# A decoder layer on one core: a third pair of feed-forward blocks by two levels of Strassen products, and down's weight sums made by accumulating loads

## The chip, the cores and the metric

The kernel runs on one core of a Trainium2 chip. The metric is the device time of one execution in microseconds (us). The kernel before has a median of 2212.78 us over three runs (2210.60 to 2213.64). The profile is of one execution that took 2210.64 us; its span, from the first to the last profiled instruction, is 2208.9 us.

The engines are TensorE (PE; its weight loads are listed as PEld), VectorE (DVE), ScalarE (ACT), GpSimd (POOL) and SyncE (SP). DMAs are issued by SP, POOL and ACT, each from a queue of its own that is served in order.

## The reference

Input x is 16 batches of 128 tokens by 1024 channels in float32. Three residual steps follow each other, each on a layer norm of x:

```python
x = x + _L0_attn_ref(_layernorm(x), Wqkv, bqkv, Wo, bo)             # self attention, width 256
x = x + _L0_xattn_ref(_layernorm(x), ctx, ctx, Wq, Wk, Wv, Wo, ...) # 8 heads of 64
x = x + _L0_ffn_ref(_layernorm(x), gate, up, down ...)              # 1024 -> 2752 -> 1024
# the last one:
Wg, Wu, Wd = dequantize(gate...), dequantize(up...), dequantize(down...)
h = silu(x @ Wg.T) * (x @ Wu.T)
return h @ Wd.T
```

The three weights of the last step are packed as two 4-bit numbers per byte, with a scale and a zero for each group of 64, and are taken out as `(w - zero) * scale`. This step is most of the work.

## The kernel before, in words

**Stages.** Self attention runs to about 249 us of the span, cross attention to about 750 with a tail of small pieces up to about 802 that lies among the products of the first feed-forward block. Then comes gate and up for the second half of the batches ("pass 0", to 1266), gate and up for the first half ("pass 1", to 1728.5), and the down stage for all tokens (to 2200.7).

**Blocks.** The 2752 inner columns are ten full blocks of 256 (0 to 9) and a last one, RB = 10, of 192. A pass has 1024 tokens.

**One level.** `one_block` (L1205, with `products`, L1167) multiplies a block by a Strassen-Winograd scheme: halves of the block's columns, of the 1024 channels and of the tokens, so 7 products for gate and 7 for up in place of 8 each. A product is four matmuls of 128x128 by 512 columns. The seven sums of weights are made beforehand (`prepare`) and stored in device memory; the seven sums of tokens (`T`) lie in SBUF.

**Two levels.** `two_levels` (L1414) takes two neighbouring blocks, a pair, and applies the scheme once more inside each of the seven outer products: 49 multiplies for a pair, gate and up together, each four matmuls of 128x128 by 256 columns. The inner sums of weights (`li`) are made by GpSimd (`inner_left`, L1392), the inner sums of tokens (`ti`) by VectorE (`inner_right`, L1362), and results are combined by VectorE from PSUM (`got`). In pass 0, `PAIRS = [3, 4]` (L1095): blocks 0 to 5 go by one level, then pairs 3 and 4 (blocks 6 to 9) by two. In pass 1 all five pairs go by two levels. RB goes by one level in both passes.

**Preparation.** `prepare` (L215 to L296) is a generator that unpacks weights: it loads raw bytes, splits the nibbles, subtracts the zero, multiplies by the scale (tile `pa`, 128x1024, two buffers), makes four combinations with VectorE (`comb`, tile `pc`) and stores seven 256 KB tiles per block and matrix. For down, the matrix "d" of a block, it makes four combinations too (L275 to L284) and stores all seven sums, in the order DOWN, which is also the order of the outer products of the down stage: 1, 2, 6, 5, 3, 7, 4. Steps of the generator are taken by hand: function `beside` (L1631 to L1664) is called at each of a one-level block's fourteen products, and `between` at each outer product of a pair. Raw loads and stores go by a `Route` (L55), whose engine is changed by hand: GpSimd's queue from the start of the feed-forward, SP's from the start of the last one-level block before the pairs.

**Order.** The order of work on an engine is that of the code, except that helpers of class `InOrder` (L65) pin their own instructions among each other and a scheduler places the others around them by priority. The trace gives all instructions of such a helper one line, L73, so tiles are told by name.

**Cross attention's moves.** Query tiles are turned by VectorE (`kt`), written by SP to device memory (`kd`, L856) and read back in another layout by SP (`qs`, L861); normalised rows are written to `xt` (`turn_rows`, L589). `project_out` multiplies by `qs`, takes squares (`sq`) on ScalarE, adds them up on TensorE (`mm<-sq,ones`), and VectorE makes the norm (`y<-sq,y`) and adds it to X. VectorE's chain is in order, so `h<-p,k` of block 0 stands behind it.

**The down stage.** For each of seven outer products `oq`, `operands` (L1026) loads by SP the sums of h (`lq`) and, by `load_right` (L1037), the sums of down's weights: for kc = 0 the five even blocks (pool wq0, 5 buffers), for kc = 1 the odd ones (pool wq1, 10 buffers). `remainder` (L1746) loads RB's (`wr`). They are prefetched while the outer product before is multiplied. `combine` (L1756) makes inner sums on VectorE (`lc`, `wc`): sums of number 5 need the even tiles alone, at inner product 7 of the outer product before; number 6 the odd ones too, at inner product 3; number 7 both. The inner order is 1, 5, 6, 7, 3, 4, 2, and VectorE's results `iu` and `iv` free the PSUM banks of 6 and 5. `got` (L1788) adds up.

Of the kernel before, what the change touches and what calls it, by code (L numbers as in the profile page):

```python
# [18 lines left out]
P = 128  # L19
# [19 lines left out]

GATE = (1, 7, 6, 2, 5, 4, 3)  # L40
DOWN = (1, 2, 6, 5, 3, 7, 4)
BLOCKS = [(b * 2 * P, min(P, (INTER - b * 2 * P) // 2)) for b in range(-(-INTER // (2 * P)))]


# [32 lines left out]
def decoder_layer(  # L77
# [137 lines left out]
    def prepare(jobs, ahead, queue, vector=nc.vector, sync=nc.sync, loads_first=False):  # L215


        units = [(blk, mat, s) for blk, mat in jobs for s in range(1 if mat == "r" else 2)]
        loads = deque(load_raw(*u, sync) for u in units[:ahead])
        stores = deque()  # L220
        if loads_first:
            yield

        def put():
            while stores:
                queue.dma_start(*stores.popleft())

        for k, (blk, mat, s) in enumerate(units):
            size = [BLOCKS[blk][1] if mat == "d" else P, 512]

            if s == 0:
                A = {}
            put()
            raw, scale, zero = loads.popleft()
            if k + ahead < len(units):
                loads.append(load_raw(*units[k + ahead], sync))

            pair = pools["a"].tile([P, 2, 512], F32, name="pa")[: size[0]]
            for n, ops in enumerate(
                (  # L240
                    (4, 15, ALU.logical_shift_right, ALU.bitwise_and),
                    (15, None, ALU.bitwise_and),
                )
            ):
                A[(n, s) if mat == "d" else (s, n)] = pair[:, n]
                nib = pair[:, n].bitcast(I32)
                vector.tensor_scalar(
                    nib if mat == "d" else nib.rearrange("p (j f) -> p j f", j=JC), raw, *ops
                )
            if mat != "d":  # L250
                pair = pair.rearrange("p n (j f) -> p (n j) f", f=P)
            vector.tensor_tensor(pair, pair.bitcast(I32), zero, ALU.subtract)
            vector.tensor_tensor(pair, pair, scale, ALU.mult)
            yield
            if mat == "r":
                out = wprep[blk, mat] = dram.tile([2, *size], F32, name="wr0", tag="wr0")
                for n in range(2):
                    stores.append((out[n], A[0, n]))
            if s == 0:
                continue  # L260
            put()
            out = wprep[blk, mat] = dram.tile(
                [7, *size], F32, name=f"w{mat}{blk}", tag=f"w{mat}{blk}"
            )

            def store(q, t):
                stores.append((out[(DOWN if mat == "d" else GATE).index(q)], t))

            def comb(a, b, op):
                t = pools["c"].tile([P, 512], F32, name="pc")[: size[0]]  # L270
                vector.tensor_tensor(t, a, b, op)
                return t

            store(1, A[0, 0])
            if mat == "d":  # L275
                store(3, A[1, 1])
                store(2, A[1, 0])
                put()
                t1 = comb(A[0, 1], A[0, 0], ALU.subtract)
                store(5, t1)  # L280
                t2 = comb(A[1, 1], t1, ALU.subtract)
                store(6, t2)
                store(7, comb(A[1, 1], A[0, 1], ALU.subtract))
                store(4, comb(A[1, 0], t2, ALU.subtract))  # L284
            else:
                store(4, A[1, 1])
                store(2, A[0, 1])
                put()
                s1 = comb(A[1, 0], A[1, 1], ALU.add)
                store(5, s1)  # L290
                s2 = comb(s1, A[0, 0], ALU.subtract)
                store(6, s2)
                store(7, comb(A[0, 0], A[1, 0], ALU.subtract))
                store(3, comb(A[0, 1], s2, ALU.subtract))
            yield
        put()  # L296

# [252 lines left out]

    tensor, vector = InOrder(tc, nc.tensor), InOrder(tc, nc.vector)
    sync = InOrder(tc, nc.sync)

# [35 lines left out]
    def turn_rows(b, xn, pool):  # L589

        kt = pool.tile([P, 4, 2 * JC, Q], F32, name="kt")
        vector.transpose(
            kt.rearrange("p c m t -> p m c t"), xn.rearrange("p m (c i) -> p m c i", c=4)
        )
        xt = xt_all[PASSES.index(b - b % HB)][b % HB]
        for a in range(4):
            sync.dma_start(
                xt[a].rearrange("c i n j t -> i c (n j t)"),
                kt[ts(a, Q)].rearrange("i c m t -> i c (m t)"),
            )  # L600
# [53 lines left out]
    if True:  # L654
# [163 lines left out]
        def query_unit(b, pair, qs, wait):  # L818
# [26 lines left out]
            def turn():  # L845
                kt = bkt.tile([P, 4, NB, Q], F32, name="kt")
                vector.transpose(
                    kt.rearrange("p c n j -> p n c j"),
                    qe.rearrange("p h d -> p (h d)").rearrange("p (n c j) -> p n c j", c=4, j=Q),
                )  # L850
                kd = dram.tile([4, Q, 4, NB, Q], F32, name="kd", tag="kd", bufs=3)
                sync.dma_start(kd.rearrange("a i c n j -> (a i) c n j"), kt)

                def load():
                    qt = qs[pair] = bqs.tile([P, 4, NB, Q], F32, name="qs", tag="qs")
                    for c in range(4):  # L856
                        sync.dma_start(
                            qt[ts(c, Q)], kd[:, :, c].rearrange("a i n j -> i a n j")
                        )

                later(1, load)  # L861
# [174 lines left out]

    def load_right(oq, kc, wb):  # L1037
        for i in range(NI):
            t = wb[kc, i] = pools[f"wq{kc}"].tile([P, 512], F32, name="wq")
            nc.sync.dma_start(t, wprep[2 * i + kc, "d"][DOWN.index(oq)])  # L1040

    def direct(lb, wb, L, W):

# [12 lines left out]
    with ExitStack() as gs:  # L1056
# [18 lines left out]
            banks.append(pool("c_u", 4, space=PSUM, side="right"))  # L1075

        cxb = rest = None
        route.engine = nc.gpsimd
        flagged = []


# [10 lines left out]
            return [[(2 * i + f, mat, q) for mat in "gu"] for q in DOWN for f in range(2)]  # L1092


        PAIRS = [3, 4]  # L1095
        order = [blk for blk in range(RB) if blk // 2 not in PAIRS]
        order.insert(2 * PAIRS[0], None)
        to_load = deque([t for blk in order[: 2 * PAIRS[0]] for t in tiles_of(blk)])
# [315 lines left out]
        def two_levels(ps, pairs, operands, between=lambda i, q: None):  # L1414
# [13 lines left out]
            def do_extra(n, more=0):  # L1428
                for todo, k in ((right, n), (extra, more)):
                    for _ in range(min(k, len(todo))):  # L1430
                        todo.popleft()()

            state = {}
            hs = {}
            sums = {}
# [98 lines left out]
            for n, (i, q) in enumerate(OUTERS):  # L1534
# [22 lines left out]
                if ps == 0 and q == 3:  # L1557
                    extra.extend(operands.inner_right(OUTERS[n + 2][1]))
                if ps == 1 and n == 0:
                    extra.append(lambda: outer_operand(operands.T, 4))  # L1560
                elif ps == 1 and n == 4:
                    extra.extend(operands.inner_right(4))
                multiply(n, 2)
                got(n, (0, 0), 2, 1)
                multiply(n, 5)
# [65 lines left out]
        def beside(n, mat, q):  # L1631
# [35 lines left out]
        for blk in order:  # L1667
            if blk is None:
# [11 lines left out]
                T1.update({1: pass1[0, 0], 2: pass1[1, 0], 3: pass1[1, 1]})  # L1680
                continue
            if blk == 2 * PAIRS[0] - 1:
                route.engine = nc.sync
# [31 lines left out]
    with ExitStack() as dst:  # L1715
# [30 lines left out]
        def remainder(oq):  # L1746
# [41 lines left out]
        def got(oq, ib, src, add=None, extra=None):  # L1788
# [11 lines left out]
            if oq == 4 and add is None:  # L1800

                for i in range(BPT):
                    v(m[:, i], src[:, i], u[:, i], ALU.add)
                    bs, cols = place(oq, ib)
                    outs.append((out[bs.start + i, :, cols], m[:, i]))
                    put_outs(nc.scalar if i % 2 == 0 else nc.sync)
# [10 lines left out]
            else:  # L1817
                if oq == 7:
                    v(u, src, u, ALU.add)
                v(m, src, w if oq in (3, 7) else u, ALU.add)  # L1820
            if add is not None:
                if oq == 5:
                    p(w, w, u, ALU.add)
                elif oq in (6, 7):
                    p(u, u, m, ALU.add)
                if oq in (3, 7):
                    p(m, m, w, ALU.add)
                elif oq == 2:
                    p(m, m, u, ALU.add)
                elif oq == 4:  # L1830
                    v(m, m, u, ALU.add)
            if xt is not None:
                p(m, m, xt, ALU.add)
            if oq in (2, 3, 7, 4):
# [142 lines left out]
```

## Time and profile before

| what | us |
|---|---|
| median of three runs | 2212.78 |
| the profiled execution | 2210.64 |
| its span | 2208.9 |
| TensorE busy | 2186.6 (99%), granted clock 0.999 |
| VectorE busy | 1499.2 (68%) |
| GpSimd busy | 667.4 (30%), 0.00 in the down stage |
| ScalarE busy | 510.4 (23%) |
| pass 0, one-level blocks 1 to 5 | 240.33 |
| pass 0, two pairs | 171.4 |
| pass 1, five pairs | 424.7 |
| down stage, seven outer products | 472 |
| DMA, mean share of 16 engines, 800 to 1000 / down stage | 0.94 / 0.52 |

The stages' times are differences of starts in the chain of waits, which follows the end of the program back through what released each piece of work; it runs along TensorE nearly all the time (94%). "Landing" is the time from the issue of a DMA to its completion. Busy engines are given over the whole span; what an engine costs is only to be seen in what TensorE waits for.

### The profile page before, as it was taken

The numbers are of one execution on the slowest core, as the hardware profiler recorded it, in microseconds if no ns is written. First come the engines' busy times: TensorE is split into PE (matmuls) and PEld (weight loads), VectorE is DVE, ScalarE is ACT, GpSimd is POOL, SyncE is SP. The second block draws the span as 40 slices with busy tenths as digits, with TensorE's granted clock in tenths as the row PEclk, the third lists the DMA queues.
The fourth block names the chain that finished last, engine by engine and source line by source line (L and its number), as shares of the span: only waits on it lengthen the run. The fifth ranks groups of instructions, "written<-read, shape, count | busy, mean of one in ns | idle before, by whom it ended". The sixth has DMA issues, their size and how long they took to land.

```text
span 2208.9 us, 24417 instructions
## 1 busy us (share of the span) xinstructions
PE 2186.6 (99%) x8500; PEld 1546.9 (70%) x8500; DVE 1499.2 (68%) x2055; ACT 510.4 (23%) x688; POOL 667.4 (30%) x646
## 2 busy tenths in 40 slices
PE   8999999999999999999999999999999999999998
PEld 7556555555555544444888588888887788888887
DVE  6897578888887767764578668667676645554462
ACT  2111235665566441111121112122211000000000
POOL 5453134333333335551344234444442000000000
PEclk9999999999999999999999999999999999999999
DMA  6435447777896788996566736566575966334631
GB/s 255 160 130 188 138 143 244 221 234 232 238 296 198 222 268 273 321 316 213 189 250 231 218 131 209 174 212 206 176 229 191 330 197 197 100 118 140 213 119 40
DMA packets 257716, 450.43 MB, mean 204 GB/s; under 512 B 27632, under 2 KB 122352, under 8 KB 254384
## 3 DMA queue, kind: packets, MB, share of 16 engines
q1 hardware_dynamic: 214944, 351.23, 49.8%
q0 software_dynamic: 24336, 78.40, 10.6%
q10 hardware_dynamic: 18304, 19.14, 2.8%
q8 instruction: 70, 1.15, 0.2%
q14 instruction: 62, 0.51, 0.1%
HBM read 281.35 MB, written 166.79 MB: 203 GB/s over the span
## 4 chain that ended last, share of the span: by engine, by line
PE 94%; DVE 3%; issue 1%; ACT 0%; POOL 0%; DMA 0%; DVEq 0%; POOLq 0%
PE q L73 26%; PE po L1856 21%; PE p L73 14%; PE kq L73 10%; PE mm L73 8%; PE kx L73 5%; PE mm L412 4%; PE mm L427 2%; PE p L1184 2%; PE mm L310 1%; DVE pa L73 1%; PE tr L359 1%; DVE ti L73 1%; DVE C L73 0%; DVE pc L73 0%
## 5 line engine op out<-in xcount | busy, mean ns | idle before, releaser
L73 PE MATMUL q<-ti,li 128*128 128x256 f32 x1176 | 270.8, 380 | 1.4 <-ACT k L73 0.6
L73 PEld LDWEIGHTS q<-ti,li 128*128 128x128 f32 x1176 | 222.8, 190 | 34.2 <-ACT k L73 2.2
L841 POOL TENSOR_TENSOR qe<-qe,qrec 128x1024 f32<-128x1024 f32 x64 | 148.0, 2313 | 179.0 <-DVE qrec L73 154.9
L73 ACT COPY k<-q 128x512 f32<-128x512 f32 x147 | 85.9, 585 | 462.8 <-PE q L73 462.8
L73 PE MATMUL p<-b,w 128*128 128x512 f32 x432 | 190.1, 592 | 0.0
L1856 PE MATMUL po<-wc,lc 128*128 128x256 f32 x840 | 183.4, 379 | 0.0
L73 POOL TENSOR_TENSOR li<-w 128x512 f32<-128x512 f32 x98 | 136.3, 1392 | 145.5 <-DMA w<-wu 53.0
L1856 PEld LDWEIGHTS po<-wc,lc 128*128 128x128 f32 x840 | 159.6, 190 | 21.8
L73 PEld LDWEIGHTS p<-b,w 128*128 128x128 f32 x432 | 82.1, 190 | 102.5 <-issue 100.2
L73 PE MATMUL p<-T,w 128*128 128x512 f32 x304 | 134.7, 592 | 0.0
L1856 PE MATMUL po<-wq,lq 128*128 128x256 f32 x560 | 126.7, 379 | 0.3 <-issue 0.3
L73 PEld LDWEIGHTS mm<-qs,m_sb 128*128 128x128 f32 x512 | 97.3, 190 | 40.1 <-issue 29.4
L73 DVE STREAM_TRANSPOSE kt<-qe 128x1024 f32<-128x1024 f32 x64 | 79.4, 1240 | 63.8 <-POOL qe L841 59.6
L73 PE MATMUL kx<-ek,cxt 128*128 128x512 f32 x256 | 121.7, 598 | 0.0
L73 PE MATMUL mm<-qs,m_sb 128*128 128x256 f32 x512 | 120.8, 379 | 0.0
L73 PE MATMUL kq<-wq_sb,xn 128*128 128x512 f32 x256 | 120.2, 593 | 0.4 <-ACT qe L829 0.4
L73 PE MATMUL kq<-wk_sb,cx 128*128 128x512 f32 x256 | 120.1, 592 | 0.0
L73 DVE TENSOR_TENSOR C<-q,k 128x512 f32<-128x512 f32 x105 | 71.9, 685 | 70.0 <-PE q L73 67.7
L73 POOL TENSOR_TENSOR li<-w,li 128x512 f32<-128x512 f32 x49 | 64.5, 1317 | 179.5 <-PE q L73 171.1
L1856 PEld LDWEIGHTS po<-wq,lq 128*128 128x128 f32 x560 | 106.0, 190 | 15.9 <-issue 1.1
L412 PE MATMUL mm<-xnT,wqkv_sb 128*128 128x512 f32 (+1 forms) x320 | 112.7, 508 | 0.0
L73 DVE TENSOR_TENSOR pa<-pa,sz 128x1024 f32<-128x1024 int32 x86 | 108.8, 1265 | 2.4
(206 smaller groups left out, 3789.4 us busy)
## 6 DMA issues: line engine op xcount, KB each, us to landing
w<-wu SPq DMA_DIRECT2D x140, 256.0 KB, 3.3
lq<-h SPq DMA_DIRECT2D x140, 256.0 KB, 4.5
w<-wg SPq DMA_DIRECT2D x138, 256.0 KB, 2.8
kd<-kt SPq DMA_DIRECT2D x64, 512.0 KB, 3.6
qs<-kd SPq DMA_DIRECT2D x256, 128.0 KB, 3.4
h<-hc SPq DMA_DIRECT2D x80, 256.0 KB, 2.9
wq<-wd SPq DMA_DIRECT2D x70, 256.0 KB, 5.4
h<-h SPq DMA_DIRECT2D x60, 256.0 KB, 2.5
```

The source lines that it names most:

```text
L73: return lambda *args, **kw: self._tc.keep_in_program_order(fn(*args, **kw))
L310: tensor.matmul(ps, oT[:, d, ts(b % BPT, S)], wo_d[d][:, ts(h, 512)], start=(d == 0), stop=(d == 1),)
L359: nc.tensor.transpose(tr[:, j, :], xn[:, ts(4 * h + j, P)], ident)
L412: nc.tensor.matmul(ps[:, tokens], wqkv_sb[:, f, c, :], xnT[:, c, tokens], start=(c == 0), stop=(c == CC - 1),)
L427: nc.tensor.matmul(ps, xnT[:, c, ts(i, S)], wqkv_sb[:, 4:6, c, :], start=(c == 0), stop=(c == CC - 1),)
L841: nc.gpsimd.tensor_tensor(qe, qe, rec.unsqueeze(2).to_broadcast(wide), ALU.mult)
L1184: tensor.matmul(ps, wt[:, j, :], T[q][:, :, j], start=(first == q and j == 0), stop=(q in (2, 3, 4) and j == JC - 1), skip_group_check=True,)
L1856: nc.tensor.matmul(bank[:, i, :], l[:, ts(i, S)], w,  start=(start and c == 0 and i % 2 == 0), stop=(stop and c == len(pairs) - 1), skip_g ...
```

## The change

1. `PAIRS` becomes `[2, 3, 4]`: in pass 0, blocks 4 and 5 go by two levels as well, and blocks 0 to 3 by one.
2. The preparation of down stores only the four quarters of a block's weights, with signs so that off-diagonal ones are negated; no combinations are made and three of seven stores go. The subtraction of the zero is split in two. The generator has fewer steps (36 taken instead of 47), and the places where steps are taken change: in the last one-level block before the pairs (now block 3) two at products 10 and 12, in the first pair one at the outer product 6, and in the two other pairs six each.
3. The down stage loads the first quarter of a sum by SP into its tile and adds the others by accumulating loads issued by GpSimd (`load_sums`, `TERMS`): none for the outer products 1, 2 and 3, one for 5 and 7, two for 6, three for 4. That is seven more loads for each of 11 blocks, 77 in all. `got` subtracts where it added, because of the signs.
4. The moves of cross attention (`kd`, `qs`, `xt`) that come after the feed-forward's start go by GpSimd's queue instead of SP's (`moves`). The preparation's route changes to SP at product 7 of block 3.
5. In pass 1, the last outer operand and its inner sums are made together at the first outer product instead of at two places (n = 0 and n = 4).

```diff
+QUARTERS = ((0, 0), (0, 1), (1, 0), (1, 1))
+TERMS = {1: "0", 2: "2", 3: "3", 5: "01", 6: "310", 7: "31", 4: "3102"}
...
-            if mat != "d":
-                pair = pair.rearrange("p n (j f) -> p (n j) f", f=P)
+            if mat == "d":
+
+                for n in range(2):
+                    terms = [pair[:, n].bitcast(I32), zero[:, n]]
+                    if n != s:
+                        terms.reverse()
+                    vector.tensor_tensor(pair[:, n], *terms, ALU.subtract)
+                vector.tensor_tensor(pair, pair, scale, ALU.mult)
+                if s == 0:
+                    out = wprep[blk, mat] = dram.tile([4, *size], F32, name=f"wd{blk}", tag=f"wd{blk}")
+                for n in range(2):
+                    stores.append((wprep[blk, mat][QUARTERS.index((n, s))], pair[:, n]))
+                yield
+                continue
+            pair = pair.rearrange("p n (j f) -> p (n j) f", f=P)
...
-            if mat == "d":
-                store(3, A[1, 1])
-                store(2, A[1, 0])
-                put()
-                t1 = comb(A[0, 1], A[0, 0], ALU.subtract)
-                store(5, t1)
-                t2 = comb(A[1, 1], t1, ALU.subtract)
-                store(6, t2)
-                store(7, comb(A[1, 1], A[0, 1], ALU.subtract))
-                store(4, comb(A[1, 0], t2, ALU.subtract))
...
+    moves = Route(sync)
...
-                sync.dma_start(kd.rearrange("a i c n j -> (a i) c n j"), kt)
+                moves.dma_start(kd.rearrange("a i c n j -> (a i) c n j"), kt)
...
-                        sync.dma_start(
+                        moves.dma_start(
                             qt[ts(c, Q)], kd[:, :, c].rearrange("a i n j -> i a n j")
                         )
...
         for i in range(NI):
-            t = wb[kc, i] = pools[f"wq{kc}"].tile([P, 512], F32, name="wq")
-            nc.sync.dma_start(t, wprep[2 * i + kc, "d"][DOWN.index(oq)])
+            wb[kc, i] = pools[f"wq{kc}"].tile([P, 512], F32, name="wq")
+        load_sums(oq, [(wb[kc, i], wprep[2 * i + kc, "d"]) for i in range(NI)])
+
+    def load_sums(oq, tiles):
+        for n, term in enumerate(TERMS[oq]):
+            for t, quarters in tiles:
+                src = quarters[int(term)]
+                if n == 0:
+                    nc.sync.dma_start(t, src)
+                else:
+                    nc.gpsimd.dma_start(t, src, accum_op=ALU.add)
...
-        route.engine = nc.gpsimd
+        route.engine = moves.engine = nc.gpsimd
...
-        PAIRS = [3, 4]
+        PAIRS = [2, 3, 4]
...
+            def last_operand():
+                outer_operand(operands.T, 4)
+                extra.extend(operands.inner_right(4))
...
                 if ps == 1 and n == 0:
-                    extra.append(lambda: outer_operand(operands.T, 4))
-                elif ps == 1 and n == 4:
-                    extra.extend(operands.inner_right(4))
+                    extra.append(last_operand)
...
             if blk == 2 * PAIRS[0] - 1:
                 if n == 7:
+                    route.engine = nc.sync
                     right.extend(first_operands.inner_right(DOWN[0]))
...
             elif blk == 2 * PAIRS[0] - 1 and n > 6:
-                steps = 0
+                steps = n in (10, 12)
             else:
                 steps = n in (4, 5) if blk == 1 and mat == "g" else n % 7 < 5
-                if n in {4: (9, 10), 5: (1, 3)}.get(blk, ()):
-                    steps = 0
...
-                    lambda i, q: i > PAIRS[0] and q != 7 and next(rest, None),
+                    lambda i, q: (q == 6 or i > PAIRS[0] and q != 7) and next(rest, None),
...
-            nc.sync.dma_start(wr, wprep[RB, "d"][DOWN.index(oq)])
+            load_sums(oq, [(wr, wprep[RB, "d"])])
...
-                    v(m[:, i], src[:, i], u[:, i], ALU.add)
+                    v(m[:, i], u[:, i], src[:, i], ALU.subtract)
```

Four more places of `got` are turned from an addition to a subtraction in the same way; no instruction is added there.

More of the change, by code (lines that the diff above doesn't have):

```diff
@@ L266, in store @@
             def store(q, t):
-                stores.append((out[(DOWN if mat == "d" else GATE).index(q)], t))
+                stores.append((out[GATE.index(q)], t))
             def comb(a, b, op):
@@ L274, in prepare @@
             store(1, A[0, 0])
-            if mat == "d":
-                store(3, A[1, 1])
-                store(2, A[1, 0])
-                put()
-                t1 = comb(A[0, 1], A[0, 0], ALU.subtract)
-                store(5, t1)
-                t2 = comb(A[1, 1], t1, ALU.subtract)
-                store(6, t2)
-                store(7, comb(A[1, 1], A[0, 1], ALU.subtract))
-                store(4, comb(A[1, 0], t2, ALU.subtract))
[L285 to L294, printed above, removed]
+            store(4, A[1, 1])
+            store(2, A[0, 1])
+            put()
+            s1 = comb(A[1, 0], A[1, 1], ALU.add)
+            store(5, s1)
+            s2 = comb(s1, A[0, 0], ALU.subtract)
+            store(6, s2)
+            store(7, comb(A[0, 0], A[1, 0], ALU.subtract))
+            store(3, comb(A[0, 1], s2, ALU.subtract))
             yield
@@ L856, in load @@
                     for c in range(4):
-                        sync.dma_start(
+                        moves.dma_start(
                             qt[ts(c, Q)], kd[:, :, c].rearrange("a i n j -> i a n j")
@@ L1682, in decoder_layer @@
             if blk == 2 * PAIRS[0] - 1:
-                route.engine = nc.sync
                 first_operands.pool = deep.enter_context(
@@ L1819, in got @@
                     v(u, src, u, ALU.add)
-                v(m, src, w if oq in (3, 7) else u, ALU.add)
+                if oq in (3, 7):
+                    v(m, src, w, ALU.add)
+                else:
+                    v(m, u, src, ALU.subtract)
             if add is not None:
                 if oq == 5:
-                    p(w, w, u, ALU.add)
+                    p(w, u, w, ALU.subtract)
                 elif oq in (6, 7):
@@ L1828, in got @@
                 elif oq == 2:
-                    p(m, m, u, ALU.add)
+                    p(m, u, m, ALU.subtract)
                 elif oq == 4:
-                    v(m, m, u, ALU.add)
+                    v(m, u, m, ALU.subtract)
             if xt is not None:
```

## The prediction

> **What bounds the kernel now.** I read the page's busy shares first, then the waits of TensorE, then the chain of waits in order of time to cut the span into stages.
>
> ```profile
> span 2208.9 us, 24417 instructions
> PE 2186.6 (99%) x8500; PEld 1546.9 (70%) x8500; DVE 1499.2 (68%) x2055; ACT 510.4 (23%) x688; POOL 667.4 (30%) x646
> ...
> q0 software_dynamic: 24336, 78.40, 10.6%
> ```
>
> TensorE is busy for all but 22 us, at a granted clock of 0.999: only fewer matmuls, or a wait of it that comes or goes, can move the time. Its waits inside the span are small:
>
> ```profile
> PE p L1184 <- DVE h L73: 2.5, 1, 2.5
> PE q L73 <- ACT k L73: 0.6, 1, 0.6
> PE q L73 <- DVE ti L73: 0.6, 1, 0.6
> ```
>
> The chain (start, us, line, xcount) gives the stages: one-level blocks 1 to 5; pass 0's two pairs (from 1056.8); pass 0's last block (1228.3); five pairs (1266.0); the second last block; the down stage.
>
> ```profile
> 816.50 240.33 PE p L73 x560
> 1056.83 56.99 PE q L73 x264
> ...
> 1228.28 37.77 PE p L73 x88
> ...
> 1728.55 407.39 PE po L1856 x1886
> 2136.24 64.61 PE po L1856 x298
> ```
>
> So a one-level block takes 240.33 / 5 = 48.07 us, and a pair by two levels (1228.28 - 1056.83) / 2 = 85.7. The profiled execution took 2210.64 us, 1.7 more than its span and 2.1 less than the median shown (2212.78). The sum is made against 2210.64. A measurement tells about 0.2%, 4.4 us, from no change.
>
> **1. The third pair.** Blocks 4 and 5 cost 2 x 48.07 = 96.14 us as one-level blocks. As a pair they are 49 multiplies of four groups of 256 columns; 343.87 us of pass 1's chain and the groups' mean of 380 ns put one multiply at 1.727 us and the pair at 84.63. That is **-11.5 us**. No row speaks of another price for the same matmuls: the clock is full in all 40 slices.
>
> **2. Work that is off the path.** For each of 11 down blocks 4 combinations of 0.685 us leave VectorE (30 us) and 3 of 7 stores leave the queues (33 of 256 KB, 26 us at the 0.78 us worked out in 6). TensorE waits for neither now, so by itself this is worth 0; it is what lets the preparation fit into fewer steps (36 instead of 47), three pairs leaving fewer one-level products to lie beside. Two 128x512 subtracts for one 128x1024 add about 0.1 us per unit, under TensorE's products.
>
> **3. Block 0: the wait of 2.5 us.** TensorE stands 2.51 us at 812.80 for `h<-p,k` (ends 812.74). On VectorE that sits behind an in-order chain that was itself held by the last squares:
>
> ```profile
> 805.15 1.23 DVE L73 SCALAR_TENSOR_TENSOR y<-sq,y 128x1024 f32<-128x1024 f32 x1 [7.90 <-ACT sq L912]
> ```
>
> The changed order puts the last `qs` matmuls of cross attention at about 784 instead of 797.65, and the squares' sums 10 us earlier, because the last moves (kd, qs, xt) go from SP's queue to POOL's, ahead of SP's weight loads. Then y runs at about 798, and `h` is ready near 809.4, before 810.04, when TensorE needs it: -2.3. Against it: POOL's queue is in order, too. Its last `qe` ends at 767.0, each issue is 0.54 us, twelve `qs` loads and two `kd` stores stand in it ahead of raw(gate) and of `x_all`; by landing times of 3.4 to 3.9 us, the last `qs` lands at 782 to 783 for a need at 783.9. If one more POOL step is late, TensorE waits up to 5 us in order. Bounds -2.5 and +5; I take **-2.3**, since the rows leave 1 to 3 us.
>
> **4. Blocks 1 to 3.** Down units come earlier; each (0.74 + 2.48 + scale) takes some 5 us of VectorE for a step of 4.8, and their tile pa (2 buffers) waits for stores that land in 5.4 to 6.2 us. VectorE had 70% busy and DMA 0.94 from 800 to 1000 and TensorE still did not wait. Slack before the product that needs `h` is 2.4 us. Bounds 0 and +2; **+0.5**. SP takes the route at product 7 of block 3 instead of a whole block earlier in the preparation; the first two weight loads behind it have four tiles ahead (14 us): 0.
>
> **5. Pairs.** In pair 2 one step lies at q=6, where VectorE was idle for
>
> ```profile
> 1100.10 0.69 DVE L73 TENSOR_TENSOR V<-q,k 128x512 f32<-128x512 f32 x1 [3.32 <-PE q L73]
> ```
>
> and a step costs 3.5 to 6.2 (two `pa` operations took 4.39 at 1183 beside POOL's `li`): 0 to +1. Pairs 3 and 4 carry steps as the old pair 4 did, with VectorE at 11.2 of 12.0 us and no TensorE wait over 0.2: 0 to +2. The wait for `ti` after the first outer product (1118.30, above 0.6) stays in pass 0; in pass 1 the operand that is now made whole at n=0 moves SP's and VectorE's work from n=4: -0.8 to 0. Together **+0.8**.
>
> **6. The down stage: 77 accumulating loads.** They replace nothing on TensorE. Each sum is SP's plain load, then 1 to 3 accumulating loads on POOL, each waiting for the one before on that tile: outer products 6 (two more), 5 and 7 (one), 4 (three). POOL is idle here (0.00 busy from 1700), SP keeps the same number of loads. What waits: `wc<-wq` on VectorE, in order ahead of `iu` and `iv`, whose reads free the PSUM banks of 6 and 5 for TensorE.
>
> ```profile
> 2090.36 0.42 DVE L1769 TENSOR_TENSOR wc<-wq 128x256 f32<-128x256 f32 x1
> ...
> 2091.63 1.22 DVE L1887 TENSOR_TENSOR iu<-po,iu 128x1024 f32<-128x1024 f32 x1
> ```
>
> ```profile
> 2065.68 3.47 SPq L1040 DMA_DIRECT2D wq<-wd  x5
> ...
> 2076.66 2.75 SPq L1040 DMA_DIRECT2D wq<-wd  x5
> ```
>
> ```profile
> 2099.91 1.89 PE L1856 MATMUL po<-wr,lr 96*128 96x256 f32 x8
> 2101.64 2.32 PE L1856 MATMUL po<-wq,lc 128*128 128x256 f32 x10
> ```
>
> For product 4 the even tiles are the urgent ones. The second is issued at 2077.2 and lands 5.4 us later (`wq<-wd` row), 2082.6; with three accumulates of L each it is whole at 2082.6 + 3L. Its `wc` was at 2091.3 and has 7 us until TensorE wants the bank (2092.85 against 2099.91): 2098.3. TensorE's wait is 3 (L - 5.2). For product 6 POOL's order (odd tiles' first accumulates, their second, then the even ones) puts it at about 1804.5 + 3L (SP's odd loads, issued by 1798.5, land by 1804) against 1821.8 + 7: 3 (L - 8.0), none below 8. Products 5 and 7 have one accumulate, so 2L, over 10 us, more: none.
>
> L is in no row: bounded below by the plain POOL loads in this kernel, which land in 5.4 to 6.6 us (`wd<-pc`, `raw<-in_dq`), or by SP's 5.4; above, by doubling the worst of them, 13 us, since an accumulate reads the destination and writes it back. A second limit is bandwidth: POOL's queue moved 78.40 MB in 10.6% of the engines, 0.106 x 2208.9 / 78.40 x 0.262 = 0.78 us for 256 KB. For product 4, 21 accumulates and some ten plain loads (8 us) lie between 2071 and the tile: 2071 + 21c + 8, limit 2098.3. At c = 0.78 that is 2095.4, no wait; at 1.2 it is 2104.2, 6 us; at 1.57 (double) 14 us, and product 6 then adds 6. I take L = 6.2 and c about 1.15, nearer to the plain rows because the share here is only 0.52 over the stage (0.81 in 2060 to 2090): 3 us by L, 5 by c, so **+5**. Bounds 0 and +38 (L = 13: 23 + 15).
>
> A rule that speaks against this part: "Collectives: The Full Stack", in the section on the bandwidth ceiling, says that a reduction in DMA reads two sources, so that it delivers about half of a copy (62.28 against 32.35 GB/s). No run here shows an accumulate. By it c would be 1.57 from this trace's 0.78, and the down stage would cost +20 instead of +5: the whole change +7, slower.
>
> **Sum:** -11.5 - 2.3 + 0.5 + 0.8 + 5 = -7.5: 2210.64 - 7.5 = **2203 us**.
>
> **Rivals.**
> *A. Slow accumulates; slower than before.* One mechanism: products 4 and 6 wait for chains of two and three accumulates, which POOL serves in order. For it: nothing in the trace is shaped like it, the read of the destination may double its traffic in windows already at 0.81, and 7 us is all the slack. Against: the stage as a whole has half of DMA free. The rest of the sum is -12.5, so it decides at a wait of 12.5 us: 3 (L - 5.2) + 3 (L - 8.0) = 12.5 at L = 8.7, or c = 1.4. At L = 10 to 13: 2210.6 - 12.5 + 20 to 38 = 2218 to 2236.
> *B. All is hidden.* L of 5.2 or c of 0.85: 2210.6 - 12.5 = 2198, and 2195 if the `ti` waits of pass 1 go. For it: POOL has nothing else to do, SP's rows for 256 KB loads go down to 2.5 us.
> *C. Pass 0 gives the saving back.* Preparation in 36 steps instead of 47, at 0.94 of DMA, and a late `qs` on POOL's queue: upper bounds of 3 to 5 together +5 + 2 + 3 instead of -1.0, at +5 for accumulates: 2210.6 - 11.5 + 10 + 5 = 2214. Against: pair 4 had these densities with no wait.
> *D. The change does not do what it says*: the products of blocks 4 and 5 could stay one-level. The new order of TensorE shows 49 multiplies for them, so I give it nothing.
>
> **How the numbers follow.** Chances: forecast (2199 to 2207) 0.42; A 0.24; B 0.18; C 0.16. Faster by over 0.2% (under 2208.4): forecast and B whole, 0.07 of C: 0.67. Slower (over 2217.2): A but for 0.04 and 0.01 of C: 0.21. The rest, 0.12, is within. The range from 2195 to 2227 leaves out the longer half of A and little of B. The likeliest case alone: 2199 to 2207.
>
> **What would show it.** Pass 0's pairs last some 257 us from the end of block 3 (about 3 x 85.7), and TensorE's busy time falls by 11.5; a smaller fall means step 1 is wrong. The wait on `h` of 2.5 near 812 is gone; if `mm<-qs` waits for a DMA there, step 3 is. In the down stage, `po` waits behind VectorE's `iu` or `wc` in the outer products before 4 and 6; the DMA issues list an accumulate `wq<-wd` on POOL, whose landing is L. If it stands above 9 us, A holds. Waits of `p` or `q` on `h`, `ti` or `C` between 816 and 1240 beyond 3 us mean C.

## The result and the profile after

The changed kernel takes 2228.51 us (median of six runs, 2225.99 to 2229.46) against 2212.78 before: **slower, ratio 1.0071, 95% interval 1.0058 to 1.0084**. The forecast was 2203, with a range that ended at 2227. The profiled execution has a span of 2227.3 us, 18.4 more than before; the tables below account for these 18.4. (The medians are 15.7 apart: the profiled execution before was 2.1 under its median, this one 0.6 over.)

The page's first part, after:

```profile
span 2227.3 us, 24953 instructions
PE 2181.4 (98%) x8668; PEld 1582.2 (71%) x8668; DVE 1517.2 (68%) x2070; ACT 515.0 (23%) x694; POOL 760.5 (34%) x724
...
q0 software_dynamic: 32848, 90.27, 14.3%
```

TensorE works 5.2 us less, not 11.5 less, and its idle time has grown from 22 to 46 us. TensorE's waits say where (engine, line, what it waited for: us in total, times, longest):

```profile
PE po L1877 <- DVE iu L1908: 19.5, 2, 14.6
PE q L77 <- DVE C L77: 2.5, 2, 1.6
PE p L77 <- DVE h L77: 1.8, 2, 1.3
PE p L77 <- DVE sg L77: 1.7, 2, 1.3
```

The chain of waits in order of time (start, us, what) shows the stages, and in the down stage weight loads where there was TensorE alone:

```profile
964.34 27.64 PE q L77 x128
...
1223.98 37.77 PE p L77 x88
1261.74 423.03 PE q L77 x1960
...
1722.54 67.40 PE po L1877 x312
1791.01 5.32 DMA wq<-wd
1796.95 7.57 DMA wq<-wd
1807.37 11.22 DMA wq<-wd
1821.07 6.60 DMA wq<-wd
1829.38 237.59 PE po L1877 x1088
2067.09 5.56 DMA wq<-wd
...
2116.09 38.45 PE po L1877 x166
2154.93 64.61 PE po L1877 x298
```

Stage by stage, from the starts in the two chains (the last row ends at the span's end):

| stage | before | after | difference | forecast |
|---|---|---|---|---|
| up to the first product of gate and up | 749.45 | 751.37 | +1.9 | 0 |
| blocks 0 to 3 (before: to the pairs, less 96.14 for blocks 4 and 5) | 211.2 | 213.0 | +1.7 | -1.8 |
| pass 0's pairs (before: two, and 96.14) | 267.6 | 259.6 | -8.0 | -11.5 and most of +0.8 |
| RB, twice | 75.5 | 75.5 | 0 | 0 |
| pass 1's pairs | 424.7 | 423.0 | -1.7 | 0 to -0.8 |
| down stage and end | 480.4 | 504.8 | **+24.4** | **+5** |

The first row is no effect of the change: the runs below that differ from the changed kernel only later have their first product at 749.4 to 750.4.

**Inside the down stage.** TensorE before the outer product 4 (start, us, instructions, in brackets the idle time before):

```profile
2077.15 24.34 PE L1877 MATMUL po<-wc,lc 128*128 128x256 f32 x112
2116.09 3.78 PE L1877 MATMUL po<-wr,lr 96*128 96x256 f32 x8 [14.60 <-DVE iu L1908]
2119.66 2.90 PE L1877 MATMUL po<-wq,lc 128*128 128x256 f32 x10
2122.39 0.60 PE L1877 MATMUL po<-wr,lr 96*128 96x256 f32 x2
2122.82 2.32 PE L1877 MATMUL po<-wq,lc 128*128 128x256 f32 x10
```

The releaser named is `iu`, but it is VectorE's queue that stands: ahead of `iu` it waits for a weight tile, and before that for a load of h.

```profile
2095.43 0.69 DVE L1786 TENSOR_TENSOR lc<-lq 128x512 f32<-128x512 f32 x1 [8.12 <-DMA lq<-h]
2113.19 0.43 DVE L1787 TENSOR_TENSOR wc<-wq 128x256 f32<-128x256 f32 x1 [17.06 <-DMA wq<-wd]
...
2114.82 1.22 DVE L1908 TENSOR_TENSOR iu<-po,iu 128x1024 f32<-128x1024 f32 x1
```

GpSimd's accumulating loads of the same time:

```profile
2105.72 0.86 POOL L1058 DMA_DIRECT2D wq<-wd  x1 [0.49 <-DMA wq<-wd]
2106.99 0.86 POOL L1058 DMA_DIRECT2D wq<-wd  x1 [0.41 <-DMA wq<-wd]
2108.25 0.86 POOL L1058 DMA_DIRECT2D wq<-wd  x1 [0.39 <-DMA wq<-wd]
2109.54 0.86 POOL L1058 DMA_DIRECT2D wq<-wd  x1 [0.42 <-DMA wq<-wd]
```

Each waits for an earlier one to land, and one is issued about every 1.3 us. In a window of these alone (columns: window, length, then busy time and count of PE, PEld, DVE, ACT, POOL, then granted clock, DMA share, GB/s) nothing is left of the engines:

```profile
2104.00:2113.00 9.00, 0.00 (x0) 0.00 (x0) 0.00 (x0) 0.00 (x0) 6.04 (x7) 0.50 1.11 198
```

198 GB/s is 0.262 MB in 1.3 us: **an accumulating load of 256 KB takes about 1.3 us of all engines**. GpSimd's issues fill only 6.04 of the 9 us, so their length is not what limits the rate. In a full window of plain transfers, at the stage's start, the same engines moved 357 GB/s at a share of 1.03, which is 0.73 us for 256 KB:

```profile
1722.00:1750.00 28.00, 28.00 (x130) 24.46 (x129) 22.27 (x46) 1.61 (x2) 0.00 (x0) 1.00 1.03 357
```

This agrees with the halved rate of the Trainium skill's page "Collectives: The Full Stack" (section on the bandwidth ceiling) better than with the prediction's own choice: for collectives, the page gives 62.28 / 32.35 = 1.93 for a copy against a reduction. The ratio measured here is about 1.8.

The queues' shares from 2060 to 2116 (packets, MB, share of 16 engines):

```profile
q0 software_dynamic: 3348, 6.11, 60.1%
q1 hardware_dynamic: 3147, 5.70, 31.4%
q10 hardware_dynamic: 2112, 2.10, 12.0%
```

Over 56 us, accumulates took 34 us (1.44 us for 256 KB in this mix), SP's plain loads 18 and ScalarE's transfers (loads of the residual x and stores of the result) 7: 58 us of transfers for 56.

**The clock.** After the wait of 14.6 us, eight matmuls take 3.78 us in place of 1.89, and the next ten 2.90 in place of 2.32; the granted clock in the window above is 0.50. The wait of 4.85 us before product 6 is followed by the same 3.78 and by 2.88. So the two waits of 19.5 us cost another 1.89 + 0.58 + 1.89 + 0.56 = 4.9 us, which is the rest of the +24.4, and the reason why TensorE's busy time fell by 5.2 and not by more.

### The profile page after: what moved, and what is told of

It is laid out like the page before. It is cut to its first block, busy times and chain, and to the rows that moved or that the text cites. A ratio compares the mean times of both kernels' runs of the same rounds, so it can differ in the third digit from the quotient of the medians.

```text
span 2227.3 us, 24953 instructions
## 1 busy us (share of the span) xinstructions
PE 2181.4 (98%) x8668; PEld 1582.2 (71%) x8668; DVE 1517.2 (68%) x2070; ACT 515.0 (23%) x694; POOL 760.5 (34%) x724
## 4 chain that ended last, share of the span: by engine, by line
PE 85%; DMA 6%; DVE 5%; issue 2%; POOL 1%; ACT 0%; SPq 0%; DVEq 0%; POOLq 0%; ACTq 0%
PE q L77 28%; PE po L1877 18%; PE kq L77 10%; PE mm L77 8%; PE p L77 5%; PE kx L77 5%; PE mm L418 4%; DMA wq<-wd 3%; DVE pa L77 3%; PE p L1202 2%; PE mm L433 2%; PE mm L316 1%; DMA wd<-pa 1%; PE tr L365 1%; DMA szd<-in_dsz 1%
## 5 line engine op out<-in xcount | busy, mean ns | idle before, releaser
L77 PE MATMUL q<-ti,li 128*128 128x256 f32 x1344 | 308.9, 379 | 0.8 <-ACT k L77 0.6
L77 PEld LDWEIGHTS q<-ti,li 128*128 128x128 f32 x1344 | 255.0, 190 | 36.9 <-ACT k L77 1.3
L77 ACT COPY k<-q 128x512 f32<-128x512 f32 x168 | 98.2, 585 | 533.5 <-PE q L77 533.3
L77 POOL TENSOR_TENSOR li<-w 128x512 f32<-128x512 f32 x112 | 156.6, 1399 | 111.1 <-PE q L77 61.4
L1058 POOL DMA_DIRECT2D wq<-wd x70 | 61.3, 1022 | 371.9 <-DMA wq<-wd 351.9
L77 POOL TENSOR_TENSOR li<-w,li 128x512 f32<-128x512 f32 x56 | 73.4, 1311 | 210.3 <-PE q L77 187.6
L77 PE MATMUL p<-b,w 128*128 128x512 f32 x304 | 134.3, 594 | 3.5 <-DVE h L77 1.8
L77 DVE TENSOR_TENSOR C<-q,k 128x512 f32<-128x512 f32 x120 | 82.3, 686 | 70.2 <-PE q L77 67.7
L77 PE MATMUL q<-b,w 128*128 128x256 f32 x512 | 121.0, 379 | 0.0
L77 DVE TENSOR_TENSOR pa<-pa,sz 128x1024 f32<-128x1024 int32 x86 | 113.8, 1324 | 2.4
```

Source lines behind the costliest of these rows:

```text
L77: return lambda *args, **kw: self._tc.keep_in_program_order(fn(*args, **kw))
L1058: nc.gpsimd.dma_start(t, src, accum_op=ALU.add)
```

## The experiments

All ratios are to the kernel before.

**1. Plain loads in place of accumulating ones.**

```diff
-                    nc.gpsimd.dma_start(t, src, accum_op=ALU.add)
+                    nc.gpsimd.dma_start(t, src)
```

> The 77 accumulating loads of the down stage become plain loads of the same bytes into the same tiles, from the same queue and behind the same waits; the weight sums are then only their last terms, so the values are not down's. Theory D (demand): an accumulate takes more of the DMA engines than a plain load (1.3 us for 256 KB against 0.8), and the outer product before number 4 asks for more transfer time than it lasts. Then the waits of 14.6 and 4.9 us in the down stage shrink to under 4 together, and the time is 2205 to 2210. Rival C (chain): what costs is that each term waits for the one before and GpSimd issues them in order, at 6 to 8 us a link. Then the waits stay at 12 us or more, and the time is 2220 or above.

2208.33 us, ratio 0.9984 (0.9975 to 0.9994). The waits of the down stage are one of 3.74 us; product 6 waits no more.

```profile
2094.91 3.78 PE L1877 MATMUL po<-wr,lr 96*128 96x256 f32 x8 [3.74 <-DVE iu L1908]
2098.48 3.94 PE L1877 MATMUL po<-wq,lc 128*128 128x256 f32 x10
```

Same bytes read, same queue, same waits between links, 20 us less: theory D holds for the most of it. In the stretch before product 4 (2055 to 2095) GpSimd's queue moved 6.51 MB in 47.2% of the engines' 40 us, 0.76 us for 256 KB, where the accumulating loads took 1.44. What is left in the stage, 3.7 us and the 3.5 us of slow clock behind it (1.89 + 1.62), is what the 77 loads cost as plain ones, in chain and transfers together.

**2. No second terms at all.**

```diff
-        for n, term in enumerate(TERMS[oq]):
+        for n, term in enumerate(TERMS[oq][:1]):
```

> The 77 accumulating loads are left out, each weight tile is only its first term (the values are not down's); all else is as in the changed kernel. If the down stage's loss is theirs alone, the down stage takes 472 us again as before the change, TensorE's clock shows no dip in it, and the time is 2203 to 2205, 24.7 us under the changed kernel and some 8 to 9 under the kernel before. If a part of the loss lies elsewhere in the stage (the four quarters' layout, the subtractions), it stays above 2210.

2202.96 us, ratio 0.9964 (0.9950 to 0.9978). The down stage up to its last outer product is one stretch again, as long as before the change (407.39):

```profile
1719.67 407.39 PE po L1877 x1886
2127.52 64.61 PE po L1877 x298
```

All of the stage's loss is the 77 loads'. Without them the rest of the change is worth some -8 us by the ratio (-5 to -11), where the prediction's other terms add up to -12.5. TensorE is busy for 2175.2 us here, 11.4 less than before; 10.8 of it lie between the first product of gate and up and the end of pass 0's pairs (464.82 against 475.58).

**3. Two pairs, all else as changed.**

```diff
-        PAIRS = [2, 3, 4]
+        PAIRS = [3, 4]
...
-                steps = n in (10, 12)
+                steps = 0
...
-                    lambda i, q: (q == 6 or i > PAIRS[0] and q != 7) and next(rest, None),
+                    lambda i, q: i > PAIRS[0] and q != 7 and next(rest, None),
```

> The changed kernel with only the pairs and the places of the steps set back (blocks 4 and 5 by one level, two pairs in the first pass); quarters, accumulating loads, moves and the last operand stay as changed. The third pair is worth -11.5 us of matmuls, and the changed kernel waits 3.5 us in blocks 1 to 3 and 2.5 us in its pairs for its denser preparation. If those waits come from the denser steps, they go here, and the time is 2228.5 + 11.5 - 6 = 2234. If they come from the down units' stores themselves, they stay, and the time is 2240.

The place where the preparation's route changes goes back with the steps. 2240.69 us, ratio 1.0130 (1.0113 to 1.0147): 12.2 us over the changed kernel. This is about what the third pair's matmuls promised (-11.5), but not a clean measure of them, since the waits differ too: 5.7 us in the one-level blocks, 2.7 of slow clock behind one of them and 0.6 in the pairs, against 3.5 in the blocks and 3.5 in the pairs of the changed kernel. The second reading holds: the waits in the one-level blocks do not go with the old places of the steps.

```profile
933.92 10.57 PE L77 MATMUL p<-b,w 128*128 128x512 f32 x24 [1.63 <-DVE sg L77]
...
961.88 13.25 PE L77 MATMUL p<-b,w 128*128 128x512 f32 x24 [3.66 <-DVE h L77]
...
988.70 10.46 PE L77 MATMUL p<-b,w 128*128 128x512 f32 x24
```

These rows also show the clock. A wait of 1.63 us leaves the 24 matmuls at 10.57 us; one of 3.66 makes them 13.25. In experiment 2 a wait of 2.67 left them at 10.57; experiments 7 and 9 show that a wait shorter than that can still be followed by the slow clock.

**4. A down unit's stores at the end of its own step.**

```diff
                     stores.append((wprep[blk, mat][QUARTERS.index((n, s))], pair[:, n]))
+                put()
                 yield
```

> The changed kernel, with each down unit's two stores issued at the end of its own step and not at the start of the next. Theory S: in blocks 1 to 3 VectorE waits for tile pa (two buffers), because a unit's stores are issued a step late; with the stores earlier the waits of TensorE there (3.5 us) go, time 2225. Rival Q: the queues are full there (DMA share 0.90 to 0.99), the landing is what is late, or GpSimd's queue now stands behind VectorE and holds raw loads; then the waits stay or grow, time 2228 to 2232.

2225.73 us, ratio 1.0061 (1.0044 to 1.0078). It is the number that theory S named, and the waits in the blocks fell from 3.5 to 2.3 us. But experiments 1, 2, 5, 7 and 8, whose stores are those of the changed kernel, wait 1.9 to 2.7 us in the blocks as well, its interval and the changed kernel's overlap, and 1.8 us of the difference between the two profiles lie before the edit. So it does not decide between S and Q.

**5. The sums made in device memory during pass 1.**

```diff
+    def make_sums():
...
+            for n, jobs in enumerate((
+                [(fetch, s[7], q[3], {}), (fetch, s[5], q[0], {})],
+                [(order, s[7], q[1], add), (order, s[5], q[1], add)],
+                [(fetch, s[6], s[7], {})],
+                [(order, s[6], q[0], add)],
+                [(fetch, s[4], s[6], {})],
+                [(order, s[4], q[2], add)],
+            )):
+                todo[at + n] += jobs
...
-                if n == 0:
-                    nc.sync.dma_start(t, src)
-                else:
-                    nc.gpsimd.dma_start(t, src, accum_op=ALU.add)
+            nc.sync.dma_start(t, wprep[blk, "d"][int(TERMS[oq])] if src is None else src)
```

> The changed kernel, but the four sums of each block of down are made whole in device memory during the second pass: 44 copies from SP's queue (device memory to device memory) and 44 accumulating loads from GpSimd's (chained 7 = 3 + 1, 6 = 7 + 0, 4 = 6 + 2, 5 = 0 + 1), spread over the 35 outer products, each step one product after the one that it needs. The down stage then loads whole sums by SP as before the change. Theory D (demand): the loss came from the transfers' place, in a stretch that was full; the second pass has a DMA share of 0.44 to 0.60 over 425 us, and 44 x (0.8 + 1.3) = 92 us of transfers make it 0.82 at most. Then the down stage takes 472 us, the second pass stays at 423, and the time is 2204. Rival: the transfers hold SP's weight loads or GpSimd's sums (in order behind them) and TensorE waits in the second pass; then it is 2210 or more.

2206.41 us, ratio 0.9974 (0.9962 to 0.9985): faster than both kernels. The down stage is the old one, 407.39 and 64.61 us. Pass 1 pays part of it: its pairs take 428.3 us instead of 423.0, with waits of 1.81 and 0.99 us, at a DMA share of 0.88 (columns as above; TensorE is busy for 336.62 of 338 us). TensorE's busy time in the pairs is some 2 us longer as well, at full clock; the runs do not say why.

```profile
1347.00:1685.00 338.00, 336.62 (x1554) 294.43 (x1553) 244.44 (x289) 66.25 (x103) 185.10 (x148) 1.00 0.88 252
```

Here a sum has time until the down stage; the same kind of transfer, in a place with room. There are also fewer accumulates (44 instead of 77, since 7 is used in 6 and 6 in 4), but 44 copies more; the run doesn't part the place from the count.

**6. The same, with stores at once and the second half of a down block in tiles of the other pool.**

```diff
+            if mat == "d" and s == 1:
+                part = [pools["c"].tile([P, 512], F32, name="pc")[: size[0]] for _ in range(2)]
+            else:
+                pair = pools["a"].tile([P, 2, 512], F32, name="pa")[: size[0]]
+                part = [pair[:, n] for n in range(2)]
...
+                put()
                 yield
```

> As the run with sums made in device memory, and two edits to the preparation: a down unit's stores are issued at the end of its own step, and the second half of a down block is unpacked into two tiles of the pool of combinations (128x512, four buffers, idle in those steps) in place of the third use of the two wide buffers, so that a unit does not wait for the stores of the unit two before. The multiply by the scale is two operations there. Theory S: TensorE's waits in blocks 1 to 3 and in the pairs (3.5 + 2.5 us in the changed kernel) come from units that start late because the wide buffers wait for stores; they go for the most part, and the time is 5 us under the run without these edits, 2199. Rival Q: the queues are full there and stores and raw loads land late whatever buffer they use; then the time is within 2 us of it.

2204.01 us, ratio 0.9964 (0.9951 to 0.9978), the fastest that computes everything. Of the 5 us expected it brings 2.4, and its interval overlaps that of the run before it; in the trace, waits of `p` fall from 1.9 to 1.3 us and blocks and pairs together from 470.8 to 469.4. In experiment 9, whose preparation has the same edits, no wait of `p` is left. This leans towards S; neither theory is shown.

**7. Moves and last operand set back.**

```diff
-        route.engine = moves.engine = nc.gpsimd
+        route.engine = nc.gpsimd
...
-                    extra.append(last_operand)
+                    extra.append(lambda: outer_operand(operands.T, 4))
+                elif ps == 1 and n == 4:
+                    extra.extend(operands.inner_right(4))
```

> The changed kernel with two parts set back: the last moves of cross attention go by SP's queue again, and the last outer operand of the second pass is made in two places again (n = 0 and n = 4). By the prediction's step 3 the wait of 2.5 us on h in block 0 comes back with TensorE's last pieces some 10 us later, and by its step 5 the waits of 1.6 us at the start of the second pass come back: 2228.5 + 4 = 2232.5. If the change of queue does nothing (the pieces come early for another reason), block 0 ends as in the changed kernel and the time is 2228 to 2230.

2233.92 us, ratio 1.0096 (1.0081 to 1.0111), 5.4 over the changed kernel. The old wait is back, word for word but for the line:

```profile
PE p L1202 <- DVE h L77: 2.5, 1, 2.5
```

Its price is not the old one. The eight matmuls behind it took 3.70 us before (first row) and take 5.36 here (second row; pieces of the chain), at a granted clock of 0.50 for their first 3 us:

```profile
812.80 3.70 PE p L1184 x8
813.72 5.36 PE p L1202 x8
```

Pass 1's pairs take 424.74 us again (1263.41 to 1688.15), the 1.7 us more of the kernel before. So 2.5 + 1.7 + 1.7 us make up the difference, where 4 were expected.

**8. Even tiles first.**

```diff
+    in_order = InOrder(tc, nc.gpsimd)
...
-                    nc.gpsimd.dma_start(t, src, accum_op=ALU.add)
+                    in_order.dma_start(t, src, accum_op=ALU.add)
```

> The changed kernel with the accumulating loads kept in the order of the code, so that GpSimd serves all terms of the even tiles (which sums number 5 need first) before any of the odd ones, as the changed kernel does not for outer products 6 and 4. Theory D (demand): the 33 accumulating loads for product 4 take 1.29 us each however they are ordered; the even tiles come earlier, the odd ones later, VectorE's chain (in order) stands behind the odd ones instead, and the waits of the down stage stay at 12 us or more in all; time 2221 to 2230. Rival O (order): the even tiles were late mostly because nine loads for the odd tiles stood ahead of them; then the waits fall under 8 us, the clock's dips shrink with them, and the time is 2216 or less.

2224.06 us, ratio 1.0057 (1.0041 to 1.0072). Product 6's wait is gone, so there it was the order. Before and in product 4 the wait is cut in three:

```profile
2096.36 3.78 PE L1879 MATMUL po<-wr,lr 96*128 96x256 f32 x8 [5.08 <-DVE iu L1910]
2115.98 3.89 PE L1879 MATMUL po<-wc,lq 128*128 128x256 f32 x10 [3.92 <-DVE m L1830]
2146.39 11.11 PE L1879 MATMUL po<-wq,lq 128*128 128x256 f32 x40 [4.68 <-issue]
```

They add up to 13.7 us, and the matmuls behind each are slow. The even tiles hold TensorE for 5.1 us instead of 14.6, the odd ones and what comes after hold it later. Waits and time lie where theory D put them (12 us or more, 2221 to 2230), not where O did (2216 or less): for product 4 it is demand.

**9. Experiment 6 with the transfers of pass 1 spread otherwise** (none at outer product 3, a block every 2.4 products; the cuts below are against experiment 6).

```diff
-            at = 1 + 5 * blk // 2
+            at = 12 * blk // 5
...
-    two_levels(1, range(NI), second_operands, lambda i, q: next(made, None))
+    two_levels(1, range(NI), second_operands, lambda i, q: q != 3 and next(made, None))
```

> As the run with sums made in device memory and the two edits to the preparation, with the transfers spread over 30 of the second pass's outer products (none in product 3, where VectorE makes h), a block every 2.4 of them. That run waits 2.8 us in the second pass (1.8 and 1.0 at two places) and takes 427.8 us there against 423.0 without the transfers. If the waits come from the transfers' place beside VectorE's work at product 3, the second pass takes 425 or less and the time is 2201; if they come from the load on the queues, it stays at 427 to 428 and the time is 2204.

2206.30 us, ratio 0.9975 (0.9965 to 0.9984): no gain over experiment 6. Pass 1's pairs take 430.2 us (1255.24 to 1685.47), with a wait of 2.18 us on `ti` at 1297 in place of that on `C`. Short as it is, the matmuls behind it are slow: eight take 3.44 and the next eight 2.14 us instead of 1.89.

```profile
1297.13 3.44 PE L77 MATMUL q<-ti,li 128*128 128x256 f32 x8 [2.18 <-DVE ti L77]
1300.37 2.14 PE L77 MATMUL q<-T,w 128*128 128x256 f32 x8
```

Sparing product 3 does not remove the waits; what holds VectorE for a microsecond or two under this load stays open.

## Why the prediction was wrong

**Step 6 failed, by its size.** It had named the place (products 4 and 6), the mechanism (VectorE's `wc` in order ahead of `iu`, which frees TensorE's bank) and both limits, and the change came out slower, as rival A had it. But it took +5 where +24.4 was measured. That lies inside the step's own bounds of 0 to +38; the range of the whole left out the longer half of A. There are four reasons:

- *c.* It took 1.15 us for an accumulate because the stage's mean share was only 0.52. Measured: 1.3 where they are alone, 1.44 in the mix. A mean over a stage says nothing of the 50 us in which the transfers pile up.
- *The other transfers.* It counted ten plain loads, 8 us, in the stretch before product 4. Between the first accumulate (2072.6) and the arrival of the tile (2113), SP's and ScalarE's queues took 27.1% and 8.0% of the engines' 40.4 us, 14 us; ScalarE's queue was not in the sum at all. With 1.3 for c its formula gives 2071 + 27 + 8 = 2106 against a limit of 2098.3, a wait of 8; with 14 for the other transfers as well it gives 14, and the trace has 14.6.
- *The order of the queue.* It let the even tiles' accumulates start at 2082.6 (2084.2 here, where TensorE is 1.6 us later). Loads for the odd tiles were ahead of them in GpSimd's queue, and none began before 2087. For product 6, where the step allowed no wait below L = 8.0 us, landing took 7.8 in the median (1795 to 1832) and the wait was 4.85. Experiment 8 removes this one by order alone.
- *The clock.* All 40 slices of the page before showed full clock, and its longest wait past the start, 2.51 us, cost only itself. In these runs every wait from 3.66 us on was followed by slow matmuls, which cost 1.8 to 3.5 us more. Of those between 2 and 2.7 us, four (2.07, 2.25, 2.51 and 2.67) left the clock full and two (2.18 and 2.51, in experiments 9 and 7) cost 1.8 and 1.7 us more. In the changed kernel the two long waits cost 4.9 us more in this way. The Trainium skill's page "TensorE: Matmul & The Clock Gate", in its part on the clock gate, has half rate after an idle window of about 3.4 us; the waits from 3.66 us on agree, and those of 2.18 and 2.51 us show that a shorter wait of TensorE is not always safe. The prediction did not weigh the clock.

For rival A's thresholds (L = 8.7, c = 1.4) the same holds: the measured landing of 8.2 (the median of the whole stage) and 1.3 lie under both, and under the 9 us that was to be A's sign, and yet it decided, because the thresholds were worked out with those omissions. That the time lies among A's 2218 to 2236 is in part luck: they were worked out for L = 10 to 13.

**Step 1 was right to within 0.7 us.** By experiment 2 the third pair takes 10.8 us from TensorE, against 11.5: it had put a pair at 84.63 us from pass 1, and TensorE is busy for 85.3 us in each pair of pass 0 (256.01 us for three). **Step 2** was right in that nothing is gained by the work removed; but experiment 3 shows waits of 5.7 us in one-level blocks that had none past block 0 before. By the code, the combinations that went took an early `put()` of the stores with them; that this is the cause is not shown. **Step 3** was right: experiment 7 brings the 2.5 us back, and the late `qs` that it feared didn't come. **Step 4** (+0.5, at most +2) was too low: blocks 1 to 3 wait 3.5 us, and 1.9 to 2.7 in the other runs with the same stores. VectorE's rows there wait for stores of `pa` to land, as the step feared (11.0 us in all between 815 and 965), but they did so before as well (9.5). **Step 5** was too low for the pairs: of 11.5 us, 8.0 arrive, with waits of 0.4 and 0.6 us in pair 2 and of 1.6 and 0.9 us on `C` in pairs 3 and 4, whose steps were said to be as light as before; pass 1 gave 1.7 where at most 0.8 was allowed.

So without step 6's loss the change is worth some 8 us (experiment 2), and with the sums made elsewhere 6 to 8 are kept (experiments 5 and 6, by medians and ratios).

## What to carry to other kernels

Price a transfer in the stretch where it must land, not by the stage's mean share: add up every queue's transfer time between the moment when the first can start and the deadline, and compare it with that length. Work that leaves an idle engine for an idle queue is still put on the same DMA engines; give it a place with slack before it is needed. And a wait of TensorE can cost more than its length: every one from 3.66 us on did here, and so did two of six between 2 and 2.7 us.

## What the runs showed that had not been expected

- An accumulating load of 256 KB occupied the DMA engines for 1.3 us where such loads were alone, a plain one in a full stretch for 0.73; GpSimd spends 0.86 us on its issue, against 0.54 for a plain one.
- TensorE's matmuls ran at about half their pace after every wait of 3.66 us and more (granted clock 0.50), and after two of the six between 2 and 2.7 us: the length of such a wait alone did not tell. After a long wait the first eight matmuls of 256 columns took 3.78 us instead of 1.89.
- A wait cut into three cost more than whole, since the clock fell three times: before product 4 one wait of 14.6 us cost 17.1 with its slow clock; in experiment 8 three of 13.7 us in all cost 21 (1.89 + 1.59, 1.57 + 0.26 and 2.3 us of slow clock behind them).
